# Layer 1's parameters moved behind the experts, the first expert tile's third product moved forward, and one more step in the routing

## The chip, the cores and the metric

The kernel runs on one NeuronCore of one Trainium2 chip. The core has a matrix engine (TensorE, PE in the profile; PEld is its weight load, which overlaps the matmuls), a vector engine (DVE), a scalar engine for activations (ACT), a general engine (POOL) and an engine that mostly issues transfers (SP). Each runs its own stream of instructions in order and waits for the others by semaphores; sixteen DMA engines move data. The metric is device time of one execution in microseconds (us); lower is better.

## The reference

Two layers over 3327 rows of 256 features, with a given 0/1 adjacency matrix. Shortened:

```python
def layer(x, adj):
    x = x + attention(layernorm(x), adj)      # softmax over the neighbours of each row
    x = x + feed_forward(layernorm(x))
    return x

# layer 0: attention with two heads of 128; feed_forward is a mixture of 16 experts:
logits = x @ gate_w + gate_b                  # the two best experts of each row, and their weights
y = sum over the two:  weight * ((silu(x @ w1[e]) * (x @ w2[e])) @ w3[e])    # hidden width 512

# layer 1: attention with one head of 256 (wh = x @ W, scores from wh @ a), then elu;
# feed_forward is a recurrence of 30 steps:
h = h + 0.01 * tanh(h); h = h * sigmoid(h); h = layernorm(h) * ln_w + ln_b; h = h @ W.T + b
```

## The kernel before

The rows stand in 26 tiles of 128 (`NT`), on SBUF for the whole run (`x`). The stages follow each other on the core:

1. **Start** (to about 80 us): loading, and `project` for layer 0: the rows are normalized, turned (transposed, L147) and multiplied with the attention's matrices (L162).
2. **Attention of layer 0** (`attend`, to about 394 us). The row tiles go in five groups, `groups0`, of 4, 6, 6, 6 and 4 tiles, once for each of two heads: ten parts. Each part runs over the 26 columns j. For each column ACT makes `e` (L276), DVE makes `pT` from it (L281), and PE multiplies (L286, one product for each row tile of the group). `work` has three buffers of `e` and `pT`.
3. **Routing**, within the attention. When a group has both heads, `route` normalizes its rows (statistics L115 and L116, variance L118, the power -1/2 on POOL in L120, the rows in L127), writes them to a table in DRAM (L516), turns them (L147, copied by ACT in L148), multiplies with the gate (L523) and picks two experts for each row with a long run of small DVE operations (L538 to L584). Two small products (L567, L568) give each row its place, and POOL scatters the rows' numbers into the experts' lists (L589). `route` is a generator: `attend` takes one step of it per column of the next parts (the variable `closing`), so each `yield` is a place where one column's work stands before the rest of the routing in the program. After it `later` holds what is still to do, a scatter every second column.
4. **Experts** (`work_off`, about 394 to 749 us). The first 61 tiles of 128 listed rows (`ALWAYS`) are worked off one after another; six more stand in an `If`. A tile s has its rows gathered by POOL (L754), turned (L819, copied by ACT in L820), multiplied with w1 and w2 (L828, 16 products), passed through SiLU on ACT (L860) and the product on DVE (L864, `made`), multiplied with w3 (L871), scaled on DVE (L874) and scattered by POOL into `given` (L875). The third product of tile s-1 stands after the first two of tile s. Three sets of weights (`SETS`) are filled in turn by SP (L793, L794, L795), each piece as soon as PE has left it; in this stage `aside` also finishes the last group's closing and routing.
5. **Layer 1's parameters**, within the experts: `layer1_parameters` issues their loads at tile 16 (`FIRST`), `score_vectors` runs at tile 22, `without_mean` (two products L135, two DVE operations L137, which take the mean out of the matrix `wv1`) at tile 26, `recurrence_parameters` (products L802 and L810, DVE operations L805, L806, L809, L812 and L813, which make `bb` and `wc` for the recurrence) at tile 30.
6. **Layer 1's attention** (about 757 to 1090 us). `add_results` loads what the experts gave for each row from `given` (L954, SP, buffers `th`, `z`, `zT` of two each) and adds it to `x` (L957, DVE). `project` then takes statistics, turns the raw rows and multiplies with `wv1` (L147, L162); ACT scales the result with rstd into `s_wh` (L968). Three groups of results are asked for at once, the others as the groups before are taken up. A memset (L943) puts ones into a column of `wh`. Then `attend` runs again, with groups of three tiles.
7. **Recurrence** (about 1090 us to the end), which uses `wc` and `bb`.

A tile framework places the instructions: it keeps the dependences and gives each engine one fixed order, in which it may move an instruction ahead of others of the program; `keep_in_program_order` holds one in its place. PSUM banks (four named `bank` in stages 1 to 5, then two, and the `acc` banks) and the buffers of the pools set how far an engine may run ahead.

Of the kernel before, what the change touches and what calls it, by code (L numbers as in the profile page):

```python
# [11 lines left out]
F32 = mybir.dt.float32  # L12
# [4 lines left out]
ALU = mybir.AluOpType  # L17
# [3 lines left out]
P = 128  # L21
# [9 lines left out]
def gat_moe_gat_recurrent_ffn(ctx: ExitStack, tc: tile.TileContext, a: dict, out: bass.AP):  # L31
    nc = tc.nc
    N, D = a["x"].shape
    KD = D // P
# [315 lines left out]
    given = dram.tile([2 * NP + SLOTS * P, D], F32, name="given")  # L350
# [31 lines left out]
    with ExitStack() as moe:  # L382
# [25 lines left out]
        def bank():  # L408
            return ps.tile([P, 512], F32, name="bank")
# [100 lines left out]
        def route(ts):  # L510
# [4 lines left out]
            here = slice(t0 * P, (t0 + n) * P)  # L515
            nc.scalar.dma_start(table_x[here, :].rearrange("(t p) d -> p t d", p=P), row[:, :n, :])  # L516
            yield
            pg = bank()[:, : n * E].rearrange("p (j e) -> p j e", e=E)
            for j0 in range(0, n, 2):
                hT = turned(row[:, j0 : j0 + 2, :], turn, ps)  # L520
# [273 lines left out]
            nc.sync.dma_start(w2, a["w2"][bass.ds(e, 1)].rearrange("e (k p) h -> p (e k) h", p=P), **kw)  # L794
            behind = nc.sync.dma_start(w3, a["w3"][bass.ds(e, 1)].rearrange("e (f p) o -> p (e f) o", p=P), **kw).ins  # L795

        def recurrence_parameters():


            pb = bank()[:, :D]  # L800
            for k in range(KD):
                nc.tensor.matmul(  # L802
                    pb, lhsT=lb[:, k : k + 1].to_broadcast([P, P]), rhs=fW[:, k, :], start=(k == 0), stop=(k == KD - 1)
                )
            nc.vector.tensor_tensor(bb, pb, fb, ALU.add)  # L805
            nc.vector.tensor_scalar(bb, bb, S, None, op0=ALU.mult)  # L806
            pc = bank()[:, :D]
            for k in range(KD):
                nc.vector.tensor_scalar(wc[:, k, :], fW[:, k, :], lw[:, k : k + 1], None, op0=ALU.mult)  # L809
                nc.tensor.matmul(pc, lhsT=ones_r, rhs=wc[:, k, :], start=(k == 0), stop=(k == KD - 1))  # L810
# [25 lines left out]

        ahead = deque()

        def work_off(s0, s1, aside):

            hT = features_first(ahead.popleft())
            made = None
            for s in range(s0, s1 + 1):
                if s == FIRST:
                    for _ in aside:
                        pass
                    layer1_parameters()
                if s == FIRST + 6:
                    score_vectors()
                if s == FIRST + 10:  # L850
                    without_mean(wv1, D + 2, ones_r, bank())
                if s == FIRST + 14:
                    recurrence_parameters()
                hidT = made
                if s < s1:
                    if s + 4 < s1:
                        ahead.append(gathered(s + 4))
                    pa = product(hT, ew[s % SETS][0])
                    act = edge("e")
                    nc.scalar.activation(act, pa, AF.Silu)  # L860
                    next(aside, None)
                    pb = product(hT, ew[s % SETS][1])
                    made = edge("pT")
                    nc.vector.tensor_tensor(made, act, pb, ALU.mult)  # L864
                    if s + 1 < s1:
                        hT = features_first(ahead.popleft())
                if s > s0:
                    w3 = ew[(s - 1) % SETS][2]
                    po = ps_o.tile([P, 512], F32, name="acc1")[:, :D]
                    for f in range(FH):  # L870
                        nc.tensor.matmul(po, lhsT=hidT[:, f, :], rhs=w3[:, f, :], start=(f == 0), stop=(f == FH - 1))  # L871
                    y0 = 6 * KD * HID + s % 2 * D
                    y = sets[1][:, y0 : y0 + D]
                    nc.vector.tensor_scalar(y, po, weight[:, s - 1 : s], None, op0=ALU.mult)  # L874
                    put = nc.gpsimd.indirect_dma_start(  # L875
                        out=given, out_offset=bass.IndirectOffsetOnAxis(ap=to[:, s - 1 : s], axis=0), in_=y,
                        in_offset=None,
                    )
                    tc.declare_no_dep(put.ins, group="given", reason="no two results have the same row")
                    tc.add_to_no_dep_group("given", put.ins)  # L880
                if s + SETS - 1 < s1:
                    weights(s + SETS - 1)
                next(aside, None)
# [53 lines left out]
    with ExitStack() as st:  # L937
# [2 lines left out]
        s_wh = keep.tile([P, NT, 1, D + 3], F32, name="s_wh")  # L940
        wh = s_wh[:, :, :, 2:]
        sc = Scores(keep, 1, s_wh[:, :, 0, 0:2].rearrange("p t (s h) -> p t s h", h=1))
        nc.vector.memset(wh[:, :, :, D : D + 1], 1.0)  # L943
        work = st.enter_context(tc.tile_pool(name="work2", bufs=2))
        ps_o = st.enter_context(tc.tile_pool(name="ps2o", bufs=2, space=PSUM))
        names = cycle(("th", "z", "zT"))
# [1 line left out]
        def add_results(some):  # L948
            for ts in some:
# [6 lines left out]
                for k in range(2):  # L956
                    nc.vector.tensor_tensor(here, here, two[k], ALU.add)  # L957

        add_results(groups1[:3])
        count = 1  # L960

        def spot():
# [163 lines left out]
```

## Time and profile before

| | us |
|---|---|
| median of 3 runs | 1951.39 |
| lowest and highest run | 1948.05, 1952.37 |
| the profiled execution's own time | 1949.34 |
| its span in the trace | 1947.6 |

| stage (us of the span) | PE busy | DVE busy | ACT busy | POOL busy | mean PE clock granted | share of DMA |
|---|---|---|---|---|---|---|
| attention, 159.3 to 238.4 | 77.51 of 79.1 | 64.68 | 56.28 | 14.00 | 1.00 | 0.39 |
| attention, 238.4 to 317 | 77.01 of 78.6 | 64.47 | 55.96 | 16.10 | 1.00 | 0.38 |
| experts, 394 to 470 | 71.07 of 76 | 25.86 | 14.41 | 36.36 | 0.96 | 0.92 |
| experts, 470 to 721 | 250.42 of 251 | 57.47 | 43.47 | 86.17 | 1.00 | 0.93 |
| end of the experts and start of layer 1, 721 to 800 | 64.72 of 79 | 36.99 | 30.79 | 14.42 | 0.91 | 0.46 |

How to read it. The span runs from the first to the last instruction that the profiler recorded; the execution's own time has 1.7 us more around it. PE is busy for 97% of the span, but the ends of matmuls are modelled, so a busy PE can be a slow one; its clock can be granted at half, which a column of the windows view shows. A float32 matmul of the program appears as two records. A row of the timeline has its start and its length in us, the engine, the line, the operation, what it writes and reads, the number of instructions merged into it, and in brackets how long the engine idled before and what ended that wait. An engine name with q (POOLq, PEldq) is the engine's sequencer, which waits, branches and issues.

### The profile page before, as it was taken

Reading aid. Unit: us, or ns where it says so; the run is one execution under the profiler, and the core shown is the slowest. Engines: PE = TensorE matmul, PEld = TensorE weight load, DVE = VectorE, ACT = ScalarE, POOL = GpSimd, SP = SyncE. Lnnn points to the kernel's source line nnn. Section 1 sums busy time; section 2 is a strip of 40 time slices with the busy share of each in tenths; the row PEclk is TensorE's granted clock in tenths of the full one; section 3 lists DMA queues with packets and bytes.
Section 4 is the critical chain, followed back from the end, with each engine's and each line's share of the span. In section 5 each row is a group of like instructions: output and inputs, shape, how many; then the busy total and the mean of one; then the engine's idle time right before and its main releaser. Section 6 shows DMA issues by size and latency. Waiting matters only on the chain.

```text
span 1947.6 us, 33722 instructions
## 1 busy us (share of the span) xinstructions
PE 1897.3 (97%) x11987; PEld 1743.4 (90%) x11987; DVE 1279.9 (66%) x3828; ACT 1101.2 (57%) x1593; POOL 940.4 (48%) x864
## 2 busy tenths in 40 slices
PE   7999999999999997999999999999999999999998
PEld 6999999998999996888888888888888888888887
DVE  6888788832222224577766777777777777777778
ACT  2977766721111112656655666666666666666664
POOL 3020203244333331001000388888888888888886
PEclk9999999999999998999999999999999999999999
DMA  8978051089999975000000100000000000000003
GB/s 169 117 107 108 17 87 47 21 284 290 346 318 328 303 263 187 9 21 13 17 21 11 36 1 1 1 1 1 1 1 1 1 1 1 1 1 1 1 1 119
DMA packets 140947, 158.61 MB, mean 81 GB/s; under 512 B 52169, under 2 KB 100556, under 8 KB 140778
## 3 DMA queue, kind: packets, MB, share of 16 engines
q1 hardware_dynamic: 124657, 123.57, 20.3%
q0 software_dynamic: 11440, 28.09, 8.5%
q10 hardware_dynamic: 4680, 4.76, 0.7%
q8 instruction: 98, 1.61, 0.3%
q14 instruction: 72, 0.58, 0.1%
HBM read 166.09 MB, written 29.80 MB: 101 GB/s over the span
## 4 chain that ended last, share of the span: by engine, by line
PE 73%; issue 9%; POOL 5%; DVE 4%; DMA 2%; ACT 0%; SPq 0%; another core or an unknown queue 0%; POOLq 0%; DVEq 0%
PE po L1055 35%; PE acc L286 24%; PE bank L1040 9%; DVE pT L281 2%; PE bank L828 2%; POOL given L875 2%; POOL rb L754 2%; DMA given<-wh,to 2%; PE acc L871 1%; PE bank L523 1%; PE acc L162 0%; DMA z<-given 0%; POOL rstd L120 0%; PE bank L147 0%; DMA th<-given 0%
## 5 line engine op out<-in xcount | busy, mean ns | idle before, releaser
L1055 PE MATMUL po<-wc,zT 128*128 128x256 f32 x3120 | 692.9, 380 | 0.0
L1055 PEld LDWEIGHTS po<-wc,zT 128*128 128x128 f32 x3120 | 584.5, 190 | 76.4
L1031 POOL TENSOR_TENSOR th<-th,x 128x1024 f32<-128x1024 f32 (+1 forms) x210 | 460.8, 2216 | 101.3 <-ACT th L1029 99.7
L276 ACT ACTIVATE e<-rb,minus,full 128x384 f32<-128x384 f32 (+3 forms) x494 | 400.1, 824 | 180.2 <-DVE pT L281 162.0
L281 DVE SCALAR_TENSOR_TENSOR pT<-e,part,adjT 128x384 f32<-128x384 f32 (+3 forms) x494 | 380.5, 774 | 134.2 <-PE acc L286 114.4
L1037 DVE BATCH_NORM_STATS2 stats<-z 128x6 f32<-128x256 f32 x780 | 273.7, 412 | 147.8 <-ACT z L1032 147.8
L1061 DVE SCALAR_TENSOR_TENSOR x<-po,rr,bb 128x256 f32<-128x256 f32 x780 | 321.0, 473 | 59.0 <-PE po L1055 57.3
L1050 ACT COPY zT<-bank 128x512 f32<-128x512 f32 x390 | 201.0, 598 | 269.9 <-PE bank L1040 269.9
L286 PE MATMUL acc<-wh,pT 128*128 128x129 f32 x2704 | 310.3, 276 | 1.6 <-DVE pT L281 1.6
L286 PEld LDWEIGHTS acc<-wh,pT 128*128 128x128 f32 x2704 | 305.2, 192 | 2.2 <-DVE pT L281 2.0
L286 PE MATMUL acc<-s_wh,pT 128*128 128x257 f32 x1352 | 294.7, 380 | 2.8 <-DVE pT L281 2.7
L286 PEld LDWEIGHTS acc<-s_wh,pT 128*128 128x128 f32 x1352 | 256.1, 190 | 41.1 <-DVE pT L281 5.2
L120 POOL TENSOR_TENSOR rstd<-ve,neg_half 128x4 f32<-128x4 f32 (+3 forms) x28 | 30.8, 1099 | 390.1 <-DVE ve L118 306.6
L1020 POOL TENSOR_TENSOR rr<-rr,neg_half 128x4 f32<-128x4 f32 (+1 forms) x210 | 209.5, 997 | 17.5
L1032 ACT ACTIVATE z<-th 128x1024 f32<-128x1024 f32 (+1 forms) x210 | 200.8, 1019 | 1.3 <-POOL th L1031 1.3
L1029 ACT ACTIVATE th<-x 128x1024 f32<-128x1024 f32 (+1 forms) x210 | 199.2, 1010 | 1.3 <-DVE x L127 1.3
L1040 PE MATMUL bank<-ident,z 128*128 128x128 f32 x1560 | 187.7, 273 | 1.6 <-DVE high L988 1.6
L1040 PEld LDWEIGHTS bank<-ident,z 128*128 128x128 f32 x1560 | 177.0, 141 | 12.4 <-ACT zT L1050 1.8
L864 DVE TENSOR_TENSOR pT<-e,bank 128x512 f32<-128x512 f32 x61 | 41.9, 687 | 182.3 <-PE bank L828 123.2
L828 PEld LDWEIGHTS bank<-hT,wh 128*128 128x128 f32 x1280 | 152.3, 195 | 7.5 <-issue 3.2
L828 PE MATMUL bank<-hT,wh 128*128 128x128 f32 x1280 | 153.5, 279 | 4.9 <-issue 2.8
L860 ACT ACTIVATE e<-bank 128x512 f32<-128x512 f32 x61 | 36.4, 597 | 194.7 <-PE bank L828 99.3
(192 smaller groups left out, 1328.4 us busy)
## 6 DMA issues: line engine op xcount, KB each, us to landing
wh<-in_w_dram SPq DMA_DIRECT2D x120, 512.0 KB
first_set<-in_w_dram SPq DMA_DIRECT2D x63, 512.0 KB
in_bytes<-in_adj_dram POOLq DMA_DIRECT2D x3, 2496.0 KB
x<-in_x_dram SPq DMA_DIRECT2D x6, 512.0 KB
kept<-x SPq DMA_DIRECT2D x8, 384.0 KB
old<-kept SPq DMA_DIRECT2D x6, 512.0 KB
out_dram<-x SPq DMA_DIRECT2D x6, 512.0 KB
table_x<-row ACTq DMA_DIRECT2D x3, 768.0 KB
```

What stands on the lines that cost most here:

```text
L276: nc.scalar.activation(e[:, : n * P], rb[:, : n * P], AF.Relu, scale=sc.full[:, j, h : h + 1], bias=sc.minus[:, j, h : h + 1],)
L281: masked = nc.vector.scalar_tensor_tensor(pT[:, : n * P], e[:, : n * P], sc.part[:, j, h : h + 1], adjT[:, j // 2, ts[0] * P : (ts[-1] + 1 ...
L286: nc.tensor.matmul(po[c], lhsT=pT[:, c * P : (c + 1) * P], rhs=wh[:, j, h, :], start=(j == 0 and c % per_bank == 0), stop=(j == NT - 1), s ...
L828: nc.tensor.matmul(p[:, f, :], lhsT=w[:, k, f * P : (f + 1) * P], rhs=hT[:, k, :], start=(k == 0), stop=(k == KD - 1),)
L1020: nc.gpsimd.tensor_tensor(r[:, :n], r[:, :n], neg_half[:, :n], ALU.pow)
L1031: nc.gpsimd.tensor_tensor(th[:, :n, :], th[:, :n, :], hs, ALU.add)
L1032: nc.scalar.activation(z[:, :n, :], th[:, :n, :], AF.Silu, scale=1.0 / S)
L1037: nc.vector.bn_stats(stats[:, j, :], z[:, j, :])
L1040: nc.tensor.transpose(pt[j // 2][:, j % 2, k, :], z[:, j, k * P : (k + 1) * P], ident)
L1050: nc.scalar.copy(zT[:, 2 * c : 2 * c + 2, :, :], pt[c])
L1055: nc.tensor.matmul(po[:, j, :], lhsT=zT[:, j, k, :], rhs=wc[:, k, :], start=(k == 0), stop=(k == KD - 1),)
L1061: nc.vector.scalar_tensor_tensor(x[:, ts[0] + j, :], po[:, j, :], rr[:, j : j + 1], bb, op0=ALU.mult, op1=ALU.add)
```

## The change

There are four edits.

- `route` yields once more between writing the rows to the table and turning them, for every row group but the last.
- `without_mean` and `recurrence_parameters` leave the experts' loop. They stand behind the `If`, ahead of `add_results`, and take their PSUM banks from layer 1's pool (two buffers) instead of the experts' (four).
- The third product with its scaling and scatter becomes a function, `results`. For the first tile it is called ahead of the second tile's first product; for all the others it stands where it was.
- The memset of `wh`'s ones moves from ahead of `add_results` to behind its first three groups, and keeps its place in the program's order.

```diff
@@ route
             nc.scalar.dma_start(table_x[here, :].rearrange("(t p) d -> p t d", p=P), row[:, :n, :])
             yield
+
+            if ts is not groups0[-1]:
+                yield
             pg = bank()[:, : n * E].rearrange("p (j e) -> p j e", e=E)
@@
-        def recurrence_parameters():
+        def recurrence_parameters(bank):
@@
+        def results(s, hidT):
+
+            w3 = ew[s % SETS][2]
+            po = ps_o.tile([P, 512], F32, name="acc1")[:, :D]
+            for f in range(FH):
+                nc.tensor.matmul(po, lhsT=hidT[:, f, :], rhs=w3[:, f, :], start=(f == 0), stop=(f == FH - 1))
+            y0 = 6 * KD * HID + s % 2 * D
+            y = sets[1][:, y0 : y0 + D]
+            nc.vector.tensor_scalar(y, po, weight[:, s : s + 1], None, op0=ALU.mult)
+            put = nc.gpsimd.indirect_dma_start(
+                out=given, out_offset=bass.IndirectOffsetOnAxis(ap=to[:, s : s + 1], axis=0), in_=y, in_offset=None
+            )
...
@@ work_off
                 if s == FIRST + 6:
                     score_vectors()
-                if s == FIRST + 10:
-                    without_mean(wv1, D + 2, ones_r, bank())
-                if s == FIRST + 14:
-                    recurrence_parameters()
                 hidT = made
+                if s == 1:
+
+                    results(0, hidT)
...
-                if s > s0:
-                    w3 = ew[(s - 1) % SETS][2]
...
+                if s > max(s0, 1):
+                    results(s - 1, hidT)
@@ layer 1
         sc = Scores(keep, 1, s_wh[:, :, 0, 0:2].rearrange("p t (s h) -> p t s h", h=1))
-        nc.vector.memset(wh[:, :, :, D : D + 1], 1.0)
...
+        without_mean(wv1, D + 2, ones_r, ps.tile([P, 512], F32, name="bank"))
+        recurrence_parameters(lambda: ps.tile([P, 512], F32, name="bank"))
         add_results(groups1[:3])
+        tc.keep_in_program_order(nc.vector.memset(wh[:, :, :, D : D + 1], 1.0))
```

Nothing is computed differently: the same operations on the same data, in another order.

More of the change, by code (lines that the diff above doesn't have):

```diff
@@ L837, in gat_moe_gat_recurrent_ffn @@
         ahead = deque()
+        def results(s, hidT):
[9 more added lines that the diff above has]
+            )
+            tc.declare_no_dep(put.ins, group="given", reason="no two results have the same row")
+            tc.add_to_no_dep_group("given", put.ins)
         def work_off(s0, s1, aside):
@@ L866, in work_off @@
                         hT = features_first(ahead.popleft())
-                if s > s0:
-                    w3 = ew[(s - 1) % SETS][2]
[L869 to L880, printed above, removed]
+                if s > max(s0, 1):
+                    results(s - 1, hidT)
                 if s + SETS - 1 < s1:
```

## The prediction

> **What bounds the kernel now.** I read the chain of waits first. Its row by line gives PE 73% of the span and the attention line L286 and the recurrence line L1055 most of it, so the kernel is PE-bound except where the chain leaves PE. Then I took the waits of PE stage by stage, because an edit is worth only what the stage that it touches can give.
>
> Layer 0's attention (100 to 394 us). PE has no wait there except behind routing. The timeline around the second row group's routing:
>
> ```profile
> 189.20 0.17 DVE L118 TENSOR_SCALAR ve<-mv 128x6 f32<-128x6 f32 x1
> 189.52 1.99 POOL L120 TENSOR_TENSOR rstd<-ve,neg_half 128x6 f32<-128x6 f32 x1 [42.25 <-DVE ve L118]
> 191.55 2.03 DVE L127 TENSOR_SCALAR row<-x,mv,rstd 128x256 f32<-128x256 f32 x6 [1.26 <-POOL rstd L120]
> 192.10 0.67 PE L147 MATMUL bank<-ident,row 128*128 128x128 f32 x4 [1.32 <-DVE row L127]
> ```
>
> PE runs in program order. The turn L147 stands in front of attention products whose pT is ready, and PE stands still for 1.32 us until the normalized row exists. The waits view has this wait four times: 1.1, 1.3, 1.3 and 1.2 us for row groups 0 to 3.
>
> The experts (394 to 749 us). PE is busy for 250.42 of the 251 us from 470 to 721. The chain's marks for every third tile show the beat:
>
> ```profile
> 538.86 2.72 issue
> 555.41 3.59 issue
> 572.84 2.72 issue
> 591.12 2.72 issue
> 607.68 2.71 issue
> ```
>
> Three tiles take 16.55 us (538.86 to 555.41, and 591.12 to 607.68), but 17.43 and 18.28 us in between. In those two stretches stand the layer-1 parameters:
>
> ```profile
> 551.88 1.03 PE L135 MATMUL bank<-wv,ones_r 128*128 128x258 f32 x4
> 574.83 1.03 PE L802 MATMUL bank<-fW,lb 128*128 128x256 f32 x4
> 575.69 1.03 PE L810 MATMUL bank<-wc,ones_r 128*128 128x256 f32 x4
> ```
>
> Between the experts and layer 1 nothing can run but the last scatter and the loads that wait for it:
>
> ```profile
> 750.09 0.97 POOL L875 DMA_INDIRECT given<-wh,to  x1 [0.76 <-DVE wh L874]
> 754.31 0.38 SPq L954 DMA_DIRECT2D th<-given  x1
> 757.19 0.69 DVE L957 TENSOR_TENSOR x<-x,th 128x512 f32<-128x512 f32 x1 [2.42 <-DMA th<-given]
> 758.80 1.09 PE L147 MATMUL bank<-ident,x 128*128 128x128 f32 x4 [9.50 <-DVE x L957]
> ```
>
> PE idles for 9.5 us there. After it, layer 1's front (757 to 797 us) is a relay: loads, DVE's additions, statistics, POOL's power, PE.
>
> **The change part by part.**
>
> 1. *One more yield in `route`* (groups 0 to 3). In the changed program's order of instructions, 144 attention products stand ahead of the first turn of row groups 1 and 2 instead of 141, and 262 instead of 258 for group 0; group 3's first turns keep their place, since there the pieces of `begin_tiles` already fill the steps. A product is two records of 27.94/250 = 0.112 us (chain, 209.08), so 0.22 us. Three of them put 0.67 us of ready work into the 1.32 us wait, four put 0.89 into 1.08. The wait of 0.20 us ahead of the first L523 (for ACT's hT) falls to about 0.05. What is late next: DVE makes no pT from 190.29 to 193.49 while it writes rows, so the next is there at 194.50; by my count PE still has products of the column before until 194.9 and doesn't run dry. Behind the turns, L567 waits for `tmp`, a DVE chain of 7.10 us from L538 (199.62 to 206.72). PE has 24 products and six L243 after its last L523 before, 30 and one after: 6.9 us both times, so its wait of 0.26 us stays. Gain 0.67 + 0.15 = 0.8 us each for groups 1 and 2. In group 0 L243 moves ahead and only 20 products, not 37, stand between L523 and L567, so L567 and L568 wait perhaps 0.6 us more: 1.1 - 0.6 = 0.5 us. Together **-2.1 us**; bounds 0 (all comes back at L567) and -3.0 (0.9 of every group and no new wait). POOL's list scatters and SP's queue keep their order; each scatter hangs on the same pT as before.
>
> 2. *Parameters out of the experts.* Excess over the beat: 17.43 - 16.55 = 0.88 and 18.28 - 16.55 = 1.73, that is **-2.6 us**, all on PE. It is kept only if weights arrive in time: see the rivals.
>
> 3. *Parameters in the gap.* They come before the additions on PE and DVE. Here a rule speaks against the change. The trace first, from the branch line's view (the columns are shortest, median and longest ns, then first and last start):
>
> ```profile
> L925 PEldq COMPARE_BRANCH  x1: 3947/3947/3947, 747.3 to 747.3; - x1
> L925 DVEq COMPARE_BRANCH  x1: 76/76/76, 750.0 to 750.0; - x1
> ```
>
> The Trainium skill ("Runtime: NRT & Kernel Launch", Instruction fetch mechanics) says that a taken branch whose target isn't among the prefetched instructions stalls the engine until they are fetched, so work right behind the `If` does not get the whole gap. By the row PE restarts at 751.3, DVE at 750.2. From 751.3: a pair such as L802 takes 0.86 us at full clock (574.83 to 575.69); at the half clock that a row below shows, 1.7. L137 (0.76) lies beside L802; bb (L805 0.42, L806 0.52) follows: 751.3 + 1.7 + 1.7 + 0.9 = 755.6, against 757.19 when the first addition starts. Cover 1.6 us: cost 0. By the rule alone, with no time in it and every engine stalled, DVE too would start late; were the fetch 9.5 us on PE, the additions would start some 4 us late. I take the row.
>
> Two pairs are not covered: the order puts L812 and L813 (0.73 + about 0.4 = 1.14 us, 576.79 to 577.93) behind the first addition and ahead of the second, z, which is ready at 757.96. z slips by 1.1 us, and PE's first turn with it. DVE then idled 1.52 us for zT until 761.17; now statistics that filled 758.68 to 759.65 come after zT, so DVE, nearly full until 778, stays 1.1 us behind. What is on the path later is rstd of the third group (L118 at 776.30) and PE's wait of 1.56 us for ACT at 779.0; the fourth group's rstd, 783.34, stands about where it was by my count, since its L118 moves ahead of work. So of 1.1 us I take half, **+0.5**; bounds -0.5 (the additions now stand ahead of statistics, so loads are asked for sooner) and +3 (the first rstd, about 4 us later, holds up ACT).
>
> Does the gap's work keep PE's clock up? The windows view, with PE's busy time first and the granted clock behind POOL's:
>
> ```profile
> 756.00:758.00 2.00, 0.00 (x0) 0.00 (x0) 0.74 (x2) 0.00 (x0) 0.00 (x0) 0.50 0.91 308
> 764.00:766.00 2.00, 1.99 (x8) 1.70 (x9) 2.00 (x6) 0.59 (x1) 0.00 (x0) 0.50 1.11 352
> ```
>
> The clock is 0.50 until 766. "TensorE: Matmul & The Clock Gate" (Part 1: The HAM clock gate) has PE fall to half rate after an idle window of about 3.4 us. By the rule work at 751 to 755 might postpone the fall; but 3.5 us of idleness follow again, and PE waits for data at 779 anyway. By either, 0.
>
> 4. *First tile's third product earlier.* PE's order has three of the second tile's first products, then L871, then the rest. Its operand `made` was ready at 400.84 in the trace, and PE would reach L871 at about 401.1: the same work in another order, 0. It frees w3 at about 403.7 instead of 407.26, so SP loads the fourth tile's w3 3.6 us earlier and what queues behind it sooner; PE waits for no weight that this trace names, so 0 again. Not shown by the trace: the stall of 2.1 us and the half clock (32 records in 5.47 us at 400.05 against 3.73 us elsewhere) that stand here could vanish or repeat: 5.47 - 3.73 = 1.7 us either way, taken as 0.
>
> 5. *The memset* behind additions instead of first on DVE, where it waited for the scatter until 754.70: it would have held the parameters up, now nothing waits for it: 0.
>
> Sum: -2.1 - 2.6 + 0.5 = **-4.2 us**. The profiled execution took 1949.34 us, so 1945.1 for its like; against the median of 1951.39 it is **1947.2 us** (-0.22%). About 0.2%, or 3.9 us, is what a measurement of this kernel can tell from no change, so the forecast lies just beyond it.
>
> **Rivals.**
>
> - *Routing gives its gain back*: the wait moves from L147 to L567 and L568, where 0.2 to 0.3 us stand now and the DVE chain has the same length. For it: group 0 loses most of its cover. Against: groups 1 and 2 keep 6.9 us. Then -2.6 + 0.5: 1949.3 us. 20%.
> - *Weights bound the experts*: DMA's share is 0.94 to 1.06 from 480 to 612 us. The 2.6 us are then spent waiting for weights. Against: the beat is 16.55 us both before and after the long stretches with the same share. Then -2.1 + 0.5: 1949.8 us. 10%. The likeliest form of a change that doesn't do what it says.
> - *The early third product holds PE up*: DVE is behind POOL's power (399.47) before it makes `made`, and the margin is 0.3 us; a wait with another half-clock window costs 0.7 + 1.7: 1949.6 us. 12%.
> - *Slower: PE's restart behind the branch.* Each further fetch of 3.95 us pushes L135. The cover of 1.6 us ends at a restart at 752.9; beyond it every microsecond delays bb, DVE's first addition and all of layer 1, and the change loses from 757.1 on (4.2 more). Two more fetches (759.2) cost 6.3 us: 1953.5 us. Against: one fetch was enough before, at the same branch. 8%, a part of it beyond +0.2%.
>
> **How the numbers follow.** Forecast 50%, own range 1944 to 1948.5. The range for 8 in 10: down to 1943.4 (attention -3.0, parameters -2.6, front -0.5, clock -1.7), up to 1952.0, which holds the first three rivals and half of the last. Faster by over 0.2% is most of the forecast and a little of the rivals, as a half-clock window can go either way: 57%; same 34%; slower 9%.
>
> **What would show it.** Right: PE's wait at L147 for L127 at 0.2 to 0.7 us in groups 0 to 2 and still 1.2 in the fourth; L567 no more than 0.9; every three tiles 16.55 us from 470 to 720; L135 starting about 4 us after PE's branch and bb done before the first addition; from the last expert product to layer 1's first pT (749.3 to 796.25 us before) 47 to 48 us. Wrong: PE waits on weights in the experts, a first addition that waits for bb, an L567 wait over 1.3 us, or a stall over 1 us ahead of L871 at the second tile.

## The result, and the profile after

The changed kernel takes 1948.11 us (median of 13 runs, 1945.21 to 1950.59), the kernel before 1952.86 us (13 runs beside it, 1948.05 to 1960.08): ratio 0.9971, 95% interval 0.9961 to 0.9981. A second set of runs, made with the last experiments, gave 0.9976 (0.9967 to 0.9985). So the change gains 0.24 to 0.29%, about 5 us, which is 0.5 to 1.5 us more than the 4.2 us that were forecast. Both intervals exclude no change; neither excludes the 0.2% that the prediction takes as the limit of such a measurement. One run of the experiment e10_recurrence_late below took 2849.64 us at a mean granted clock of 0.655 and is left out; in all other runs of the changed kernels the clock was 0.99 or more.

The two profiled executions are only 2.4 us apart (1949.34 and 1946.91 us): the one of before was 3.5 us below its median, the one of after 1.2 us. The stages show where. Each is measured between two instructions that both kernels have; "half clock" is what the trace's clock intervals show.

| stage | before | after | difference |
|---|---|---|---|
| start, to the first L286 | 52.29 | 52.19 | -0.1 |
| layer 0's attention, first to last L286 | 341.65 | 339.25 | **-2.40** |
| first eleven expert tiles, to 473.94 / 470.83 | 80.00 | 79.40 | -0.6 |
| remaining tiles, to the last expert product | 275.35 | 272.43 | **-2.92** |
| last expert product to last scatter's issue | 0.80 | 0.80 | 0 |
| last scatter to the first load from `given` | 4.22 | 6.09 | **+1.87** |
| that load to the first addition | 2.88 | 2.97 | +0.1 |
| first addition to layer 1's first pT | 39.06 | 39.31 | +0.25 |
| layer 1's attention, first to last L286 | 296.01 | 297.34 | **+1.33** |
| recurrence, and the end | 854.70 | 854.73 | 0 |

Now the lines that answer to those of before. After's code has other line numbers from `route` on: L526 is the gate product (L523 before), L570 and L571 the two small products (L567, L568), L831 an expert's first two products, L847 the third, L850 the weighting, L851 the scatter into `given`, L958 the load from it, L961 the addition, L805 the products for `bb`, L809 its last operation, L815 and L816 the last ones on `wc`, L812 the first (L809 before), L881 the product on DVE (L864). In the kernels of the experiments these are up to four lines off.

After's timeline at the second group's routing (start, length, engine, line, what is written and read, count, idle before):

```profile
188.22 1.99 POOL L120 TENSOR_TENSOR rstd<-ve,neg_half 128x6 f32<-128x6 f32 x1 [40.46 <-DVE ve L118]
190.24 2.03 DVE L127 TENSOR_SCALAR row<-x,mv,rstd 128x256 f32<-128x256 f32 x6 [1.25 <-POOL rstd L120]
190.80 0.67 PE L147 MATMUL bank<-ident,row 128*128 128x128 f32 x4 [0.65 <-DVE row L127]
...
192.19 2.91 DVE L281 SCALAR_TENSOR_TENSOR pT<-e,part,adjT 128x768 f32<-128x768 f32 x3
```

POOL and DVE are as before, PE waits 0.65 us where it waited 1.32. DVE's next pT comes only at 192.19, and PE still has products: between its turns and gate products it runs on without a gap. The waits view gives 0.2, 0.7, 0.7 and 1.2 us at L147 for the four groups (before 1.1, 1.3, 1.3, 1.2), and L570 waits 0.3 us in the first three (before 0.2, 0.3, 0.3).

After's chain of waits, every third tile (start and length; "issue" is time in which no other cause shows):

```profile
535.42 2.72 issue
551.98 2.73 issue
568.54 2.71 issue
...
585.08 2.73 issue
...
601.64 2.72 issue
```

Three tiles now take 16.55 us here (16.56, 16.56, 16.54, 16.56). The two long stretches of 17.43 and 18.28 us are gone. Weights came in time: PE's waits view names no transfer from 470 to 721 us.

One operation of `recurrence_parameters` did not move, though. The framework has put its first one on `wc`, which needs only loaded data, among the experts, right behind the issue of its loads: in before (the first line) and in after alike.

```profile
504.64 0.62 DVE L809 TENSOR_SCALAR wc<-fW,lw 128x256 f32<-128x256 f32 x2 [8.03 <-DMA lw<-in_ln_w_dram]
...
501.21 0.61 DVE L812 TENSOR_SCALAR wc<-fW,lw 128x256 f32<-128x256 f32 x2 [7.75 <-issue]
501.74 0.68 DVE L881 TENSOR_TENSOR pT<-e,bank 128x512 f32<-128x512 f32 x1
...
502.48 2.00 PE L847 MATMUL acc<-wh,pT 128*128 128x256 f32 x8 [0.26 <-DVE pT L881]
```

In before it waits for the load of `lw`; in after the wait is as long, but its row names no cause. DVE works in order, so the expert's product L881 stands behind it, and PE waits for that. This one tile took 6.37 us in before, 6.05 in after and 5.52 to 6.65 in the others, where the rest of the beat is 5.52. So 0.3 of the 2.92 us in the table is the difference in this one tile and no gain of the change. Holding that operation back could gain 0 to 1.1 us (an estimate from these times; no run tried it).

After's timeline in the gap:

```profile
741.38 1.89 PE L847 MATMUL acc<-first_set,pT 128*128 128x256 f32 x8
...
744.06 0.96 POOL L851 DMA_INDIRECT given<-wh,to  x1 [0.76 <-DVE wh L850]
745.40 1.90 PE L135 MATMUL bank<-wv,ones_r 128*128 128x258 f32 x4 [2.13 <-PEq L930]
747.10 1.91 PE L805 MATMUL bank<-fW,lb 128*128 128x256 f32 x4
...
749.50 0.29 DVE L809 TENSOR_SCALAR bb<-bb 128x256 f32<-128x256 f32 x1
750.15 0.38 SPq L958 DMA_DIRECT2D th<-given  x1
...
753.12 0.69 DVE L961 TENSOR_TENSOR x<-x,th 128x512 f32<-128x512 f32 x1 [3.32 <-DMA z<-given]
753.73 0.75 DVE L815 SCALAR_TENSOR_TENSOR wc<-bank,wc 128x256 f32<-128x256 f32 x2
754.39 0.49 DVE L816 TENSOR_SCALAR wc<-wc 128x256 f32<-128x256 f32 x2
754.79 0.69 DVE L961 TENSOR_TENSOR x<-x,z 128x512 f32<-128x512 f32 x1
755.53 1.12 PE L147 MATMUL bank<-ident,x 128*128 128x128 f32 x4 [5.61 <-DVE x L961]
```

PE starts L135 2.13 us behind its last expert product, which ends at 743.27. `bb` is finished at 749.79, and DVE then stands idle for 3.32 us until data land: the parameters hold nothing up there. Between the first and the second addition stand L815 and L816, 1.1 us, as the order of instructions had shown. The gap is nevertheless longer than before's, because SP's first load started 6.09 us behind the last scatter's issue instead of 4.22.

The clock: one more row, after's windows view (PE's busy time first, the granted clock behind POOL's).

```profile
794.00:796.00 2.00, 2.00 (x6) 1.58 (x5) 0.32 (x2) 1.38 (x3) 0.00 (x0) 0.50 0.28 98
```

At the start of layer 1's attention PE is busy and has half the clock, from 793.36 to 796.77; before had no such window. From the last expert product to layer 1's first pT it is 49.16 us, so one sign of the forecast (47 to 48 us) is missed. Whether the slower landing and this window belong to the change is what the experiments had to settle.

### The profile page after: what moved, and what is told of

Same layout as the page of the kernel before. It is cut to its first block, busy times and chain, and to the rows that moved or that the text cites. A ratio compares the mean times of both kernels' runs of the same rounds, so it can differ in the third digit from the quotient of the medians.

```text
span 1945.2 us, 33722 instructions
## 1 busy us (share of the span) xinstructions
PE 1899.3 (98%) x11987; PEld 1745.9 (90%) x11987; DVE 1278.6 (66%) x3828; ACT 1100.8 (57%) x1593; POOL 938.9 (48%) x864
## 4 chain that ended last, share of the span: by engine, by line
PE 72%; issue 9%; DVE 5%; POOL 5%; DMA 2%; ACT 0%; another core or an unknown queue 0%; SPq 0%; POOLq 0%; DVEq 0%; ACTq 0%
PE po L1063 35%; PE acc L286 23%; PE bank L1048 9%; POOL given L851 2%; DVE pT L281 2%; PE bank L831 2%; POOL rb L757 2%; DMA given<-wh,to 2%; PE acc L847 1%; PE acc L162 1%; PE bank L526 1%; POOL rstd L120 0%; PE bank L147 0%; DVE x L961 0%
## 5 line engine op out<-in xcount | busy, mean ns | idle before, releaser
L286 PE MATMUL acc<-wh,pT 128*128 128x129 f32 x2704 | 309.5, 276 | 1.6 <-DVE pT L281 1.6
L286 PEld LDWEIGHTS acc<-wh,pT 128*128 128x128 f32 x2704 | 305.0, 192 | 2.1 <-DVE pT L281 2.0
L286 PE MATMUL acc<-s_wh,pT 128*128 128x257 f32 x1352 | 296.1, 382 | 2.7 <-DVE pT L281 2.7
L286 PEld LDWEIGHTS acc<-s_wh,pT 128*128 128x128 f32 x1352 | 257.7, 191 | 40.9 <-DVE pT L281 4.8
L881 DVE TENSOR_TENSOR pT<-e,bank 128x512 f32<-128x512 f32 x61 | 41.9, 687 | 183.2 <-PE bank L831 123.1
L831 PEld LDWEIGHTS bank<-hT,wh 128*128 128x128 f32 x1280 | 150.7, 194 | 8.3 <-ACT hT L823 6.4
L831 PE MATMUL bank<-hT,wh 128*128 128x128 f32 x1280 | 151.9, 278 | 5.8 <-ACT hT L823 5.8
```

Of the source, the lines that this page charges most:

```text
L286: nc.tensor.matmul(po[c], lhsT=pT[:, c * P : (c + 1) * P], rhs=wh[:, j, h, :], start=(j == 0 and c % per_bank == 0), stop=(j == NT - 1), s ...
L831: nc.tensor.matmul(p[:, f, :], lhsT=w[:, k, f * P : (f + 1) * P], rhs=hT[:, k, :], start=(k == 0), stop=(k == KD - 1),)
```

## The experiments

Theory: the time comes from the attention's wait and the beat of the experts, and the gap hides the parameters. Rivals: routing gives its gain back; weights or the early third product take part of it; the parameters' place costs the 1.9 us in the gap or the half-clock window. All kernels were timed beside the kernel before, in three sets; its own median differs from set to set (1948.83, 1952.31, 1954.73 us), so kernels of different sets are compared by their ratios.

| kernel | median, us (runs) | before beside it | ratio (95%) |
|---|---|---|---|
| e1_yield | 1945.91 (22) | 1948.83 | 0.9985 (0.9978 to 0.9992) |
| e2_params | 1945.15 (22) | 1948.83 | 0.9981 (0.9973 to 0.9989) |
| e3_third | 1949.19 (14) | 1948.83 | 1.0004 (0.9993 to 1.0014) |
| e4_two_yields | 1954.38 (15) | 1948.83 | 1.0029 (1.0020 to 1.0038) |
| e5_memset_first | 1948.32 (13) | 1952.31 | 0.9980 (0.9971 to 0.9989) |
| e7_four_results | 1947.33 (10) | 1952.31 | 0.9975 (0.9965 to 0.9984) |
| e8_wc_ahead | 1950.22 (13) | 1952.31 | 0.9989 (0.9981 to 0.9998) |
| e9_twice | 1950.91 (13) | 1952.31 | 0.9988 (0.9978 to 0.9999) |
| e11_two_parts | 1947.57 (8) | 1954.73 | 0.9960 (0.9946 to 0.9975) |
| e12_again | 1949.54 (22) | 1954.73 | 0.9976 (0.9967 to 0.9985) |
| e10_recurrence_late | 1951.22 (21) | 1954.73 | 0.9982 (0.9973 to 0.9992) |
| e13_additions_first | 1949.41 (22) | 1954.73 | 0.9972 (0.9960 to 0.9983) |

And the stages of their profiled executions, as in the table above (us):

| kernel | attention 0 | first tiles | other tiles | scatter to load | load to addition | addition to pT | attention 1 |
|---|---|---|---|---|---|---|---|
| before | 341.65 | 80.00 | 275.35 | 4.22 | 2.88 | 39.06 | 296.01 |
| after | 339.25 | 79.40 | 272.43 | 6.09 | 2.97 | 39.31 | 297.34 |
| e1_yield | 339.18 | 77.89 | 274.51 | 6.23 | 2.73 | 38.50 | 297.71 |
| e2_params | 343.07 | 74.42 | 271.96 | 5.81 | 2.95 | 38.77 | 297.35 |
| e3_third | 341.45 | 79.81 | 274.86 | 6.13 | 2.77 | 38.08 | 297.71 |
| e4_two_yields | 342.07 | 83.12 | 272.24 | 5.66 | 2.96 | 38.93 | 296.85 |
| e5_memset_first | 339.24 | 79.20 | 271.91 | 5.27 | 2.76 | 39.21 | 295.56 |
| e7_four_results | 339.25 | 82.40 | 271.91 | 5.53 | 2.96 | 38.80 | 295.65 |
| e8_wc_ahead | 339.24 | 80.73 | 272.08 | 5.67 | 2.93 | 40.49 | 295.71 |
| e9_twice | 339.94 | 79.28 | 272.62 | 6.06 | 3.77 | 40.15 | 295.55 |
| e11_two_parts | 346.71 | 77.27 | 272.73 | 5.70 | 3.02 | 38.57 | 295.65 |
| e12_again | 340.06 | 79.51 | 273.04 | 5.42 | 2.94 | 38.91 | 295.66 |
| e10_recurrence_late | 340.81 | 86.61 | 271.91 | 5.39 | 2.88 | 40.18 | 295.93 |
| e13_additions_first | 340.07 | 79.16 | 272.19 | 5.82 | 3.01 | 39.16 | 297.24 |

**e1_yield**: the kernel before, and only this edit.

```diff
             yield
+            if ts is not groups0[-1]:
+                yield
             pg = bank()[:, : n * E]...
```

> Only the extra yield in route. Theory (three to four products fill PE's wait for the normalized row): end of the attention (experts' first products) 2.0 to 2.6 us earlier than the 393.9 us of before, L147's waits 0.2, 0.7, 0.7 and 1.2 us in the four row groups, L570 no more than 0.4 each; time -2 us (ratio 0.9985 to 0.9992). Rival (routing gives its gain back): the waits at L570 and L571 grow by what L147's lose, the experts start within 0.5 us of before, ratio 1.000.

Ratio 0.9985, that is -2.9 us, more than the -2 us expected; the 0.9985 to 0.9992 of the expectation lie within the interval. The attention takes 339.18 us, the experts start at 391.7, and the waits are 0.2, 0.7, 0.7, 1.2 at L147 and 0.3 at L570 in each of the first three groups. The rival, which has the gain come back at L570, falls.

**e2_params**: only the parameters and the memset.

```diff
-                if s == FIRST + 10:
-                    without_mean(wv1, D + 2, ones_r, bank())
-                if s == FIRST + 14:
-                    recurrence_parameters()
...
+        without_mean(wv1, D + 2, ones_r, ps.tile(...))
+        recurrence_parameters(lambda: ps.tile(...))
         add_results(groups1[:3])
+        tc.keep_in_program_order(nc.vector.memset(wh[:, :, :, D : D + 1], 1.0))
```

> Only the parameters and the memset behind the experts. Theory (2.6 us of PE work leave the full beat, and the gap hides them but for 0.5 us): every three tiles 16.55 us through 530 to 720 us, last expert product 2.6 us earlier, last expert product to layer 1's first pT at most 47.5 us, time -2 us (ratio about 0.999). Rival 1 (weights bound the experts): beat longer than 16.55 us at 550 to 590, waits of PE for weights, last expert product as before, ratio 1.000. Rival 2 (the gap does not hide them; the 2.2 us that the changed kernel lost there are theirs): from last expert product to first pT 49 us or more again, time 0 to -0.5 us.

Ratio 0.9981, -3.7 us (2.1 to 5.3), where the stages account for about 2.3 to 2.6 us. The other tiles take 271.96 us; with the parameters among them e1 took 274.51 and e3 274.86, so 2.6 us at least leave the beat, and rival 1 falls. From the last expert product to the first pT it is 48.3 us, neither the 47.5 of the theory nor the 49 of rival 2. The columns "scatter to load" and "addition to pT" settle that one: e1 and e3, which keep the parameters in the experts, have 6.23 and 6.13 us from scatter to load. The slow landing is not the parameters' doing. It was before's profiled execution, with 4.22, that was out of line: all thirteen others have 5.27 to 6.23. (Its attention, 343.07 us, has a half-clock interval at 195 us that no other has.)

**e3_third**: only `results(0, hidT)` ahead of the second tile's products (and `s > max(s0, 1)` for the others).

```diff
                 hidT = made
+                if s == 1:
+                    results(0, hidT)
...
-                if s > s0:
+                if s > max(s0, 1):
+                    results(s - 1, hidT)
```

> Only the first tile's third product ahead of the second tile's first. Theory (the same PE work in another order): ratio 1.000 within 0.0005, all marks from 470 us on within 0.5 us of before, unless the half-clock window at 400.9 to 404.3 us of before goes: then 1.0 to 1.7 us earlier from 405 us on. Rival (the early product waits for its operand and holds PE up): a wait over 1 us at the second tile's start and up to 2.4 us later.

Ratio 1.0004 (0.9993 to 1.0014): nothing. The half-clock window at 400.9 us stays in its trace, and the early product waits less than 1 us for its operand (0.9 us at the third product). The last expert product ends 1.0 us earlier than in before, a little more than the 0.5 us of the expectation; 0.5 of it lies in the other tiles.

**e4_two_yields**: the changed kernel with one more yield everywhere.

```diff
             yield
+            yield
             if ts is not groups0[-1]:
                 yield
```

> The changed kernel with one yield more: two columns' steps instead of one between rows and turns in groups 0 to 2, one in group 3. Theory (the rest of the wait at L147 is filled as the first part was): L147's waits 0 to 0.2 us in groups 0 to 2 and 0.4 to 0.7 in group 3, experts start 1.5 to 2 us earlier than the changed kernel's 391.4, time -1.5 us against it, ratio to before 0.996. Rival (the turns, now later, make tmp later than its users): L570 and L571 wait 0.5 us or more in each group, experts' start within 0.5 us of the changed kernel's.

Both expectations missed: 0.30% slower than before, with an attention of 342.07 us, 2.8 longer than the changed kernel's. The wait at L147 is gone, and L570 (L571 here) waits 0.3, 0.3 and 0.7 us. What took its place is in the timeline of the second group:

```profile
190.54 2.03 DVE L127 TENSOR_SCALAR row<-x,mv,rstd 128x256 f32<-128x256 f32 x6 [1.26 <-POOL rstd L120]
191.62 0.60 PE L147 MATMUL bank<-ident,row 128*128 128x128 f32 x4
192.49 3.80 DVE L281 SCALAR_TENSOR_TENSOR pT<-e,part,adjT 128x768 f32<-128x768 f32 x4
...
193.56 2.28 PE L286 MATMUL acc<-wh,pT 128*128 128x129 f32 x18 [1.33 <-DVE pT L281]
```

With two columns' products ahead of the turn, PE has used up what pT there was. DVE writes six rows for 2.03 us and makes no pT meanwhile, so PE stands for 1.33 us behind the turn instead of in front of it. The prediction's remark on what is late next ("doesn't run dry") holds for one yield and fails for two. In group 3, where this kernel has the one yield that the change leaves out, PE's waits around the routing sum to 3.0 us against 2.6 in after: the wait at L147 falls from 1.18 to 0.28 us, and longer or new ones for pT, ACT and `tmp` take its place. There is nothing to gain there. The rest of its loss (83.12 against 79.40 us in the first tiles) lies where the executions differ by themselves, see below.

**e5_memset_first**: the changed kernel with the memset first on DVE again.

```diff
         sc = Scores(keep, 1, ...)
+        nc.vector.memset(wh[:, :, :, D : D + 1], 1.0)
...
-        tc.keep_in_program_order(nc.vector.memset(wh[:, :, :, D : D + 1], 1.0))
```

> The changed kernel with the memset of the ones column first on DVE again, ahead of the parameters. Theory (it overwrites what the last scatter reads and waits for it, L137 behind it with PE's products): L137 starts at about 750.5 instead of 747.4, bb is done 2.4 us later, 752.9, and the first addition at 753.1 is just not held up: front at most 0.5 us longer, time 0 to +0.5 us. Rival (the wait reaches the additions): first addition 1 us or more later behind the load, time +1 to +2.5 us.

The theory's outcome held, with larger cover: L137 waits with the memset for the last scatter, but the addition doesn't.

```profile
744.86 1.11 PE L135 MATMUL bank<-wv,ones_r 128*128 128x258 f32 x4 [1.77 <-PEq L930]
...
749.53 0.43 DVE L137 SCALAR_TENSOR_TENSOR wv<-bank,wv 128x258 f32<-128x258 f32 x1 [5.92 <-DMA given<-wh,to]
...
750.66 0.30 DVE L809 TENSOR_SCALAR bb<-bb 128x256 f32<-128x256 f32 x1
...
751.92 0.69 DVE L962 TENSOR_TENSOR x<-x,th 128x512 f32<-128x512 f32 x1 [0.97 <-DMA th<-given]
```

The parameters slip by 2 us (L137 at 747.39 in after) and still end 0.97 us before the first load lands. The ratios 0.9980 here and 0.9971 and 0.9976 for the changed kernel can't be told apart.

**e8_wc_ahead and e9_twice** asked for the front and the cover. e8 pins the four operations on `wc` (L815, L816) ahead of the additions with `keep_in_program_order`, and the additions too; e9 is e8 with the two calls made twice.

```diff
-                nc.vector.scalar_tensor_tensor(wc[:, k, :], pc, ...)
+                tc.keep_in_program_order(nc.vector.scalar_tensor_tensor(wc[:, k, :], pc, ...))
...
-                    nc.vector.tensor_tensor(here, here, two[k], ALU.add)
+                    tc.keep_in_program_order(nc.vector.tensor_tensor(here, here, two[k], ALU.add))
```

> The changed kernel with the four DVE operations on wc ahead of the first addition instead of between the first and the second. Theory (they are what the front loses): first addition to layer 1's first pT 38.3 to 38.7 us, as in the kernels that keep the parameters in the experts (38.1 to 39.1), instead of 38.8 to 39.3; first addition still waits for its load alone; time -0.5 us, too little for the medians. Rival (the front doesn't feel the second addition's delay): 38.8 to 39.3 again.

> As e8_wc_ahead, with all layer-1 parameters made twice over in the gap (the second pass works on wv1 as the first left it and takes its mean once more; the rest is the same numbers again). One pass runs from about 745.4 to 750.9, the first addition's load lands 9.8 us behind the last expert product, 2.2 us later. Theory (the gap covers one pass and 2 us more): the second pass costs 5.5 - 2.2 = 3.3 us, within 1 us, against e8_wc_ahead, all of it before the first addition. Rival 1 (nothing is covered, the pass costs itself): +5.5. Rival 2 (cover larger): below 1.5.

e8 missed both expectations: 40.49 us from addition to pT, longer than the 39.31. The edit did more than it was meant to: with the additions pinned, the framework placed other operations differently among them. DVE's first variance (L118) stands behind six additions instead of five, and the first two L197, which wait for nothing in after, wait 1.24 and 0.92 us for ACT. The first of them:

```profile
769.17 0.17 DVE L197 TENSOR_SCALAR minus<-part 128x2 f32<-128x2 f32 x1 [1.24 <-ACT part L195]
```

So it says nothing on L815 and L816. e9 differs from e8 only in the second pass, though, and rival 2 of its expectation holds: the second pass costs at most 0.84 us (load to addition 3.77 against 2.93); the medians are 0.7 us apart, within their error. The expectation had taken 5.5 us for a pass by itself; but the passes overlap on PE and DVE. The first pass's last operation on `wc` ends at 751.94, the second's at 755.52:

```profile
751.66 0.28 DVE L818 TENSOR_SCALAR wc<-wc 128x256 f32<-128x256 f32 x1
...
755.23 0.29 DVE L818 TENSOR_SCALAR wc<-wc 128x256 f32<-128x256 f32 x1
755.90 0.69 DVE L963 TENSOR_TENSOR x<-x,th 128x512 f32<-128x512 f32 x1 [0.37 <-DMA z<-given]
```

The load of the first addition lands about 2.9 us after it is issued (e8's 2.93), at an estimated 752.13 + 2.93 = 755.06, so about 3.1 us of cover are left behind one whole pass. The row puts the last 0.37 us before the addition down to a load, so it may have landed later than that, and the second pass cost less than 0.84 us. The gap takes all three pairs of products and their DVE work with time to spare.

**e10_recurrence_late and e13_additions_first** tried the front again, without pinning. e10 calls `recurrence_parameters` behind `project`; e13 calls `add_results(groups1[:3])` ahead of both calls, which spreads L815 and L816 over the first three additions.

```diff
         without_mean(wv1, D + 2, ones_r, ps.tile(...))
-        recurrence_parameters(lambda: ps.tile(...))
         add_results(groups1[:3])
...
         project(groups1, wv1, D + 2, split1, work, ps, spot, ...)
+        recurrence_parameters(lambda: ps.tile(...))
```

```diff
+        add_results(groups1[:3])
         without_mean(wv1, D + 2, ones_r, ps.tile(...))
         recurrence_parameters(lambda: ps.tile(...))
-        add_results(groups1[:3])
```

> The changed kernel with the recurrence's parameters behind layer 1's projection instead of in the gap. Theory (the second addition no longer has L815 and L816 ahead of it, but the parameters now stand ahead of layer 1's first pT, on PE 1.7 us and on DVE 2.5 us, beside waits for ACT of 2 to 3 us): first addition to first pT 38.5 to 40 us, time 0 to +1.5 us against the changed kernel. Rival (gap and front are worth the same): within 0.3 us of 39.0.

> The changed kernel with the additions issued ahead of the parameters, so that the four operations on wc spread over the first three additions instead of all between first and second. Theory (the delay of the second addition is what the front pays): first addition to first pT 38.4 to 38.8 us. Rival (the front's length doesn't hang on it): 38.8 to 39.3 us. Medians within 0.1% of the changed kernel's.

e10: 40.18 us from addition to pT (0.2 above the theory's upper end) and 0.9982 against 0.9976 for the changed kernel in the same set: by the profiles the gap is the better place by about 1 us, which the medians can't confirm. e13: 39.16 us, where the rival stands. So the delay of the second addition was not shown to be what the front pays. What is shown is the size: kernels with the parameters in the experts have 39.06, 38.50 and 38.08 us (mean 38.55), those with them in the gap and nothing else altered in the front (after, e2, e4, e7, e11, e12) 38.57 to 39.31 (mean 38.88); the ranges overlap.

**e7_four_results**: the profiles of e1 to e4 show DVE's weighting waiting up to 8 us for a scatter into `given` at 430 to 460 us. In e1 the waits view of DVE has

```profile
DVE wh L877 <- DMA given<-wh,to: 7.1, 2, 6.4
```

(total, times, longest). With two buffers more for the results that wait should go.

```diff
+        more_y = hold.tile([P, 2, D], F32, name="more_y")
...
-            y = sets[1][:, y0 : y0 + D]
+            y = sets[1][:, y0 : y0 + D] if s % 4 < 2 else more_y[:, s % 2, :]
```

> The changed kernel with four instead of two buffers for the weighted results of a tile. Theory (in the first ten tiles DVE's weighting waits up to 8 us for the scatter of two tiles before, which lies behind the list scatters, and PE behind it): no wait of DVE for given between 430 and 460 us, the experts' start-up 2 to 5 us shorter, time -2 to -4 us against the changed kernel, ratio to before 0.995 to 0.996. Rival (the stall is one of all engines during the list scatters, whatever the buffers): a stall of 4 to 6 us stays, time as the changed kernel's.

The rival was right. No wait for `given` is left between 430 and 460, and PE's longest waits from 394 to 475 us are

```profile
PE bank L832 <- DMA wh<-in_w_dram: 3.0, 1, 3.0
PE bank L832 <- ACT hT L824: 2.1, 1, 2.1
```

The stall now shows up at weights and at ACT, the first tiles take 82.40 us, and the time is the changed kernel's (0.9975). The wait for the buffer was one face of a stall that stays. What causes it remains open; from 431.8 to 454.0 us POOL issues list scatters, gathers and scatters of results with pauses of only 0.3 us.

**e11_two_parts and e12_again**: e1 and e2 together without e3, and the changed kernel once more.

> Yield and parameters' move together, the third product where it was in before. Theory (the third part does nothing, the other two add): stages as in the changed kernel, layer-0 attention 339.2 us (before 341.6), from the tenth tile's end behind 470 us to the last expert product 271.9 (before 274.5), ratio 0.996 to 0.998, within 0.001 of the changed kernel's in the same call. Rival (the early third product costs at the start of the experts or helps there): more than 0.001 apart.

> The changed kernel once more, beside the others of this call. Theory (-2.4 us attention, -2.6 us beat, +0.45 us front, nothing else): ratio 0.9977 plus or minus 0.001. Rival (something more is gained that the profiles don't show): 0.997 or less, as at first.

e12 confirms the size: 0.9976. e11 has 0.9960 (0.9946 to 0.9975), 0.0016 below e12 and so beyond the 0.001 of the theory, but the intervals overlap and it has only 8 runs; e3 alone gave +0.0004. The profiles lean the same way: the four kernels without the early product have 74.42 to 80.00 us in the first tiles, the ten with it 79.16 to 86.61. But before and e2, with the same order of instructions there, are 5.6 us apart by themselves, and e3's median shows no cost. That the early product costs something is an open rival to "0"; that leaving it out makes a better version is not shown. Its profile has an attention of 346.71 us, with five waits of PE for pT that sum to 5.6 us in the last group (one of 1.4 in before), where POOL scatters the lists: it is not comparable there. The other tiles take 272.73 us.

## Why the prediction was right

1. *Yield*, predicted -2.1 us: measured **-2.40** (341.65 to 339.25; five kernels that have it take 339.18 to 339.25, four 339.94 to 340.81, and e11 the 346.71 of above). By groups, from one group's first turn to the next and to the end, the sum splits into -1.2 (80.84 to 79.64), -0.6 (79.08 to 78.46), -0.6 (79.60 to 79.02) and 0 (43.16 both times). The three products were the right size (-0.67 us at L147 predicted and measured); the 0.15 at L523 for groups 1 and 2 did not come, which makes 0.6 instead of 0.8. The mis-sized term is group 0: I had charged it 0.6 us at L567 and L568, and the wait there grew by 0.1; DVE's chain behind the last gate product took 6.2 us there (L541 at 116.51 to L570 at 122.69), not the 7.1 of group 1. About 0.2 of the 1.2 us is between executions, for e3, without the yield, has 80.64. The two errors go opposite ways, so that the sum came out within 0.3 us is in part luck.
2. *Parameters out of the beat*, predicted -2.6: **-2.6** (274.51 in e1 to 271.91 in e5, e7 and e10). The two expert tiles that carried them took 6.39 and 7.25 us; those tiles now take 5.52. What the prediction did not see is the operation on `wc` that stayed behind (L812 above).
3. *In the gap*, predicted 0 before the first addition and +0.5 in the front: 0, and +0.3 that can't be told from nothing (38.55 to 38.88, ranges overlapping). The reason given for the 0.5 is not confirmed (e13). The cover was undersized: 1.6 us by the trace of before, 3.3 us of DVE's idle time in after, because before's last scatter had landed unusually soon. It is 4.6 to 5.0 us in e2, e4, e7, e11, e12 and e13, where the products run at full clock; in after a half-clock interval lies over them. On restart the row was right: PE's branch took 3.79 us, and L135 began 2.13 us behind the last expert product (1.71 to 2.15 in all eleven traces that have it there), while DVE's branch took 0.08 us. A delay at a taken branch is what the Trainium skill ("Runtime: NRT & Kernel Launch", Instruction fetch mechanics) warns of; that PE's 3.79 us are such a fetch no row says. Here the delay stays on PE and inside the gap, none came on top of it, and the slower rival falls.
4. *Third product* and *memset*, predicted 0: 0 (e3 1.0004; e5). The half-clock interval at 400.9 us that stood in before and is gone in after is still there in e3, and one starts between 398.5 and 401.6 us in five more kernels that have the early product (e4, e5, e7, e8 and e10), so the third product didn't remove it. Its cost in the first tiles is the open point of e11 above. That the memset in its old place "would have held the parameters up" is right (2 us), but it would have held up nothing else.
5. *Clock*, predicted 0 in the gap. Half-clock intervals there sum to 13.7 us in before and in after. In eight of the other nine kernels with the parameters in the gap and not made twice they sum to 10.2, and in e1 and e3 to 17.1 and 13.7: PE's work there does seem to shorten them, but "addition to pT" is no shorter for it. The rule that the prediction quotes from the Trainium skill ("TensorE: Matmul & The Clock Gate", Part 1: The HAM clock gate), half the clock after an idle window of about 3.4 us, doesn't cover two intervals here: the one at 793.36 us in after comes behind waits of 0.34 and 1.47 us, the one at 195 us in e2 behind a wait of 1.32 us. e12 has the same two waits as after and no interval.

The sum by the stages is -2.4 - 2.6 + 0.3 = -4.7 us, against -4.2 forecast; the medians' ratios give -5.7 (3.7 to 7.6) and -4.7 (2.9 to 6.4) of some 1953 us. The measured 1948.11 us lies in the forecast's own range, 1944 to 1948.5; before itself was 1.5 us slower beside it than the 1951.39 us that the forecast starts from. The parts alone give 0.9985 x 0.9981 x 1.0004 = 0.9970. Two sums of the prediction are off: the lower end of its wide range is 1951.4 - 7.8 = 1943.6, not 1943.4, and 0.9 us in each of three groups makes 2.7, not 3.0. Neither bears on the forecast.

What the profiles alone would have told wrongly is the +1.9 us from scatter to load and the +1.3 us in layer 1's attention. Neither is the change's. The first is explained above. For the second, the five kernels whose trace has a half-clock interval of 3.4 us at the start of layer 1's attention (after, e1, e2, e3, e13) take 297.24 to 297.71 us there, those without it 295.55 to 296.01 (e4, with more waits for pT, 296.85). e1 and e3 have the window with the parameters in the experts, and e12, the same kernel as after, doesn't have it. So it comes and goes with the execution; what sets it off stays open.

## What to carry to other kernels

The 2.6 us of work that left a stretch where PE was busy without a pause were gained in full, because PE and DVE waited for a transfer where it went. How much cover is left is read from the idle row behind the moved work, not from the one ahead of it. Whether all of it has moved is read from the trace, not from the program: one operation here stayed behind and still holds up a tile. Filling a wait with work that stands behind it pays only as far as that work's own supply reaches: one column more gained 2.4 us here, two lost it all, because the engine that ends the wait also makes the filler. A difference of a few us between two profiled executions is read by stages and against further profiles of either kernel: 1.9 and 1.3 us looked like losses here, and neither was the change's.

## What was not expected of the hardware

- From the issue of the last scatter to the load that waits for it: 4.22 us in one execution, 5.27 to 6.23 in thirteen.
- The first eleven expert tiles take 74 to 87 us in fourteen traces. Most of that lies between executions: before and e2, with the same order of instructions there, have 80.00 and 74.42 us, after and e10 79.40 and 86.61. Behind them the beat is 5.52 us to the hundredth, but for the tiles that carry parameters, one of 5.87 us in e3, and the last two.
- A half-clock interval of 3.4 us in layer 1's attention costs about 1.8 us (means of 297.5 against 295.7 us, e4 left out).
- The recurrence took 854.65 to 854.76 us in eleven profiles and 856.70 to 856.72 in three (e5, e7, e13). There DVE's two L127 at its start wait 0.85 to 1.11 us for the transfer that saves `x` (`kept<-x`) and last 4.35 to 4.59 us together, against 0.72 in after. Why they do in these three executions stays open.
